# Turning the second pass's normed tiles through memory and VectorE, with both writes of a unit's attention weights issued before both reads

## Chip, cores, metric

The kernel runs on one core of one Trainium2 chip. The metric is device time in microseconds, the median of three runs of the kernel before.

## What is computed

Two layers run one after the other over 8 images of 32 x 32 positions and 512 channels, all in f32.

```python
# layer 0
x_norm = _group_norm(x, gn_scale, gn_bias).reshape(b, seq, c)
q, k, v = jnp.split(x_norm @ w_qkv + b_qkv, 3, axis=-1)      # 8 heads of 64
weight = softmax(einsum('bhld,bhsd->bhls', q * scale, k * scale))
x = x_flat + einsum('bhls,bhsd->bhld', weight, v) @ w_out + b_out
# layer 1, deformable attention; x_flat has rows of 512 positions of the turned image
q = layernorm(x, ln_g, ln_b).transpose(0, 3, 1, 2).reshape(b, h * w, c) @ wq + bq
offsets = pointwise(gelu(depthwise 7x7, stride 2, of q))     # 16 x 16 points an image
interp = grid_sample_bilinear(x, reference points + tanh(offsets))
k = v = interp.reshape(b, hg * wg, c) @ wv + bv
att = softmax((q @ mq) (k @ mk)^T) (v @ mv)                  # 8 heads, 256 keys
z = att @ mo_w + mo_b + x
out = gelu(layernorm(z, ln_g, ln_b) @ mlp_w + mlp_b) + z
```

## The kernel before, in words

The kernel has two passes. The first, up to about 2216 us of the span, is layer 0 and most of the depthwise convolution. The change is in the second pass, which is layer 1.

**Units.** The second pass has 64 units. Unit n is one pair of heads of one half image: 512 queries in four tiles of 128, against 256 keys. Four units make a half image, eight an image. `unit_steps` lists a unit's work:

- `scores`: the score matmuls (`sc<-keys,q`), the row maxima on VectorE (`nmax`), and eight exponentials on ScalarE (`e`);
- `moved`, for each of the two heads: VectorE turns the weights in 32 x 32 blocks (`sq<-e`). SP writes them to a buffer in memory (`sq_d<-sq`), and reads them back in the order in which they are the right operand (`et<-sq_d`). Before the change one head's write and read are issued together;
- `share` and `spread`: the reciprocals of the sums, sent through memory (`rs_d`, `inv`);
- `query_step`: the projection of the next unit's queries (`hat_h,wqq`) and its bias on ScalarE (`q`);
- `product`, about one unit later: the weighted values (`av<-et,vals`), and then `scale` on VectorE (`attH`).

**Back steps.** When a half image's four units are done, `back_steps` takes its four tiles through the output, one tile a unit. `fetch` and `add` bring the residual (`xr`). `joined` projects the attention (`mm<-wo,attH`), adds the residual on VectorE (`z`) and takes mean and variance (`stats`, `mv`). `norm` makes `zn`. `turned` transposes `zn` with four TensorE transposes into a PSUM tile, and ScalarE copies that to `zT` in two halves. `mlp` multiplies by `wm`, `biased` adds the bias on VectorE (`res`), `gelu` and `end` follow a unit or two later.

**Beside them.** The rest of the depthwise convolution lies in units 1 to 38: `fill` on TensorE (`mm<-wq_r,hat`), `pad` on VectorE, and taps in two lanes. Lane 0's taps (`chunk<-pad,dww`) run on VectorE, three or five to a unit; lane 1's on ScalarE and GpSimd. Once an image, `point_steps` works out the sampling corners (22 small VectorE operations, at the end of the units with n mod 8 = 3), gathers rows by GpSimd's indirect DMA, and mixes them on VectorE (`smp`, at the end of n mod 8 = 4 and 6). The keys and values of the next image follow on TensorE around n mod 8 = 7, 0 and 1.

**Order.** Every step is put down with `at(place, step)`, where a place is a unit's number and a fraction. `run_due` runs them by place, and `InOrder` keeps each engine's instructions in that order. So SP, too, issues in the order of the places, and waits at each DMA for what that DMA needs. A tile of a pool can only be written again when its last reader is done. `et` has two buffers, so a read of unit n waits for the product of unit n-1.

For a tile in the back steps the places before the change are: `joined` n+0.012, `norm` n+0.03, `turned` n+0.6, `mlp` n+1.03, `biased` n+1.0392. `moved` stands at n+0.02 and n+0.04, `share` at n+0.039, `spread` at n+0.041, `query_step` at n+0.042, `product` at n+1.1, `scale` at n+1.2. TensorE's order in a unit is therefore scores, `wo`, `wm` (of the tile before), queries, `av` (of the unit before), transposes of `zn`.

Of the kernel before, what the change touches and what calls it, by code (L numbers as in the profile page):

```python
# [9 lines left out]
F32 = mybir.dt.float32  # L10
# [7 lines left out]
P = 128  # L18
# [3 lines left out]
C = 512  # L22
NC = C // P
NT = S // P
QB = 512
NQB = S // QB
NQT = QB // P
NH = 8
HD = 64
NHP = NH // 2  # L30
GRP = 16
G = 16
NS = G * G
KS = 7
SQ = 32
NSQ = P // SQ
# [30 lines left out]
class Attention:  # L67
# [66 lines left out]
    def moved(self, u, h):  # L134

        nc, shape = self.nc, [P, NSQ, NS // P, NQT, SQ]
        sq = self.work.tile(shape, F32, tag="sq", name="sq", bufs=2)
        nc.vector.transpose(
            sq.rearrange("p s j i q -> p i (s j) q"),
            u["e"][h].rearrange("p (i b q) -> p i b q", i=NQT, q=SQ),  # L140
        )
        there = self.dram.tile([P, NSQ, NS // P * QB // NSQ], F32, tag="sq_d", name="sq_d", bufs=4)
        nc.sync.dma_start(there, sq.rearrange("p s j i q -> p s (j i q)"))
        u["et", h] = self.work.tile(shape, F32, tag="et", name="et", bufs=2)
        nc.sync.dma_start(
            u["et", h].rearrange("p r j i q -> p r (j i q)"),
            there.rearrange("(r k) s x -> (k s) r x", r=NSQ),
        )
# [93 lines left out]
def attention_then_deformable_attention(  # L242
# [30 lines left out]
    nc = tc.nc  # L273
# [4 lines left out]
    dram = ctx.enter_context(tc.tile_pool(name="dram", bufs=1, space=DRAM))  # L278
# [4 lines left out]
    ident = const.tile([P, P], F32, tag="ident", name="ident")  # L283
# [7 lines left out]
    def mm_tile():  # L291
        return ps_mm.tile([P, QB], F32, tag="mm", name="mm")
# [4 lines left out]
    def load_w(pool, w, name):  # L297
        t = pool.tile([P, NC, w.shape[1]], F32, tag=name, name=name)
        nc.sync.dma_start(t, by_chunk(w))
        return t  # L300
# [61 lines left out]
    def at(place, step):  # L362
        due.append((place, len(due), step))
# [37 lines left out]
    with ExitStack() as l0:  # L401
# [3 lines left out]
        nc = InOrder(tc)  # L405
# [46 lines left out]
        att = MovedAttention(nc, ident, ps_mm, ps_sc, ps_av, work, dram, 1)  # L452
# [336 lines left out]
        for b in range(B):  # L789
# [22 lines left out]
            for hp in range(NHP):  # L812
                for qt in range(NT):
                    n = first + hp * NT + qt
# [22 lines left out]
    with ExitStack() as l1:  # L837
        nc = tc.nc
# [22 lines left out]
        def load_small():  # L861
            with nc.allow_non_contiguous_dma(reason="small vectors onto partitions"):
                for t, v in (
                    (bvk, mk_b), (bv_c, bv), (bvv, mv_b), (bqq, mq_b), (bq_c, bq), (lng, ln_g),
                    (lnb, ln_b),
                ):
                    nc.sync.dma_start(t, v.rearrange("(c p) -> p c", p=P))

        def load_conv():
            with nc.allow_non_contiguous_dma(reason="small vectors onto partitions"):  # L870
# [222 lines left out]
        def query_step(hi, hp):  # L1093
            q = queries[hi, hp] = work.tile([P, QB], F32, tag="q", name="q")
            ps = project(lambda c: wqq[:, c, ts(hp, P)], lambda c: hat[hi][:, c, :])
            nc.scalar.activation(q, ps, AF.Identity, bias=bqq[:, hp : hp + 1])

        def tmp(name, bufs):
            return work.tile([P, C], F32, tag=name, name=name, bufs=bufs)

        def back_steps(hi, start, step, tail=False):

            b, half = divmod(hi, 2)
            xs = mid[b].rearrange("(t p e) c -> e t p c", e=2, p=P)[half]
            outs = out_tok[b].rearrange("(t p e) c -> e t p c", e=2, p=P)[half]
            xr, z, zn, zT, res = {}, {}, {}, {}, {}
            n_units = 2 * B * NHP

            def fetch(t):
                xr[t] = tmp("xr", 4)  # L1110
                nc.sync.dma_start(xr[t], xs[t])

            def add(t):
                nc.gpsimd.tensor_tensor(xr[t], xr[t], bo_row, ALU.add)

            def joined(t):
                ps = project(lambda c: attH[hi][:, c, ts(t, P)], lambda c: wo[:, c, :])
                z[t] = tmp("z", 4)
                nc.vector.tensor_tensor(z[t], ps, xr[t], ALU.add)
                stats = work.tile([P, 6], F32, tag="stats", name="stats")  # L1120
                mv = xr["mv", t] = work.tile([P, 3], F32, tag="mv", name="mv")
                nc.vector.bn_stats(stats, z[t])
                nc.vector.bn_aggr(mv[:, 0:2], stats)
                rstd(mv[:, 2:3], mv[:, 1:2], 1e-5)

            def norm(t):
                zn[t], mv = tmp("zn", 2), xr["mv", t]
                nc.vector.tensor_scalar(
                    zn[t], z[t], mv[:, 0:1], mv[:, 2:3], ALU.subtract, ALU.mult
                )  # L1130

            def turned(t):
                ps = mm_tile()
                for c in range(NC):
                    nc.tensor.transpose(ps[:, ts(c, P)], zn[t][:, ts(c, P)], ident)
                zT[t] = tmp("zT", 2)
                for half in range(2):
                    nc.scalar.copy(zT[t][:, ts(half, C // 2)], ps[:, ts(half, C // 2)])

            def mlp(t):  # L1140
                res["ps", t] = project(lambda c: zT[t][:, ts(c, P)], lambda c: wm[:, c, :])

            def biased(t):
                res[t] = tmp("res", 3)
                nc.vector.tensor_tensor(res[t], res["ps", t], bm_row, ALU.add)

            def gelu(t):
                nc.scalar.activation(res[t], res[t], AF.Gelu)

            def end(t):  # L1150
                (nc.vector if tail else nc.gpsimd).tensor_tensor(res[t], res[t], z[t], ALU.add)
                (nc.sync if tail else nc.gpsimd).dma_start(outs[t], res[t])

            for t in range(NC):
                over, eve = (start + step * t >= n_units - i and not tail for i in range(2))
                n, pair = start + step * t, start + step * (t - t % 2)

                ends = (n + 0.6, n + 1.03, n + 1.0392)
                if eve:
                    ends = (n + 0.61, n + 0.72, n + 0.73) if over else (n + 1.06, n + 1.62, n + 1.625)  # L1160
                places = (pair - 1.6, pair - 0.5), (n + 0.012, n + 0.03), ends
                if tail:
                    turn = n + 0.15 + 0.005 * (t > 0)
                    places = (n - 0.7, n - 0.6), (n, n + 0.01), (turn, n + 0.25, n + 0.26)
                steps = (fetch, add), (joined, norm), (turned, mlp, biased)
                for place, what in zip(sum(places, ()), sum(steps, ())):
                    at(place, lambda t=t, what=what: what(t))


                ends = [t - 1, t] if t % 2 and not tail else [t] if tail else []  # L1170

                for what, after in (
                    (gelu, 0.27 if tail else 0.735 if over else 1.72),
                    (end, 0.28 if tail else 0.74 if over else 2.24),
                ):
                    for i in ends:
                        at(n + after, lambda i=i, what=what: what(i))
# [4 lines left out]
        def unit_steps(n):  # L1182
            hi, hp = divmod(n, NHP)
            b = hi // 2
            u = dict(tiles=NQT, at=0, v=lambda j, h: vals[b][:, j, ds((2 * hp + h) * HD, HD)])

            def scores():
                u["q"], u["k"] = queries.pop((hi, hp)), keys[b][:, hp, :]
                u["e"] = att.scores(u)

            def scale():
                if hp == 0:
                    attH[hi] = work.tile([P, NHP, QB], F32, tag="attH", name="attH")
                att.scale(attH[hi][:, hp, :], u["inv"])

            at(n, scores)
            at(n + 0.02, lambda: att.moved(u, 0))
            at(n + 0.039, lambda: att.share(u["sums"]))
            at(n + 0.04, lambda: att.moved(u, 1))
            at(n + 0.041, lambda: u.update(inv=att.spread()))  # L1200
            last = n + 1 == 2 * B * NHP
            at(n + (1.3 if last else 1.1), lambda: att.product(u))
            at(n + (1.305 if last else 1.2), scale)
            if not last:
                at(n + 0.042, lambda: query_step(*divmod(n + 1, NHP)))

# [41 lines left out]
        def load_late():  # L1250
            nonlocal bq_row, wo, wm, bo_row, bm_row
            bq_row = load_row(wp, bq, "bq_row")
            wo = load_w(late2, mo_w, "wo")
            wm = load_w(late2, mlp_w, "wm")
            bo_row = load_row(late, mo_b, "bo_row")
            bm_row = load_row(late2, mlp_b, "bm_row")
            load_conv()
# [66 lines left out]
```

## Time and profile before

| | us |
|---|---|
| runs (median; lowest, highest) | 3404.53; 3399.92, 3406.07 |
| the profiled execution's own time | 3397.38 |
| its span, first to last instruction | 3395.7 |
| second pass, first scores to last instruction | 2216.1 to 3395.7 |
| TensorE busy / VectorE / ScalarE / GpSimd | 3298.7 / 2480.5 / 1811.4 / 1547.6 |
| granted TensorE clock, mean | 0.990 |

The profiled execution took 1.7 us more than its span, and lies 7.2 us under the median of the runs. A row of the profile's groups gives the line, engine, operation, output and inputs, the count, then busy time in us and mean ns of one, then the idle time before them and what ended it. Nearly every instruction stands under L54, the line of the recording helper, so that rows are told apart by the tiles. A matmul of 64 output rows runs beside its partner of the other 64, so the mean ns of one is more than the time until the next pair starts. That spacing is read from the timeline.

### The profile page before, as it was taken

The page shows a single profiled execution, that of the slowest core. Times are in us where ns is not written, and L with a number is a line of the kernel's source. Part 1 is how long each engine was busy: PE and PEld are TensorE (multiplying, and loading weights), DVE is VectorE, ACT ScalarE, POOL GpSimd, SP SyncE. Part 2 cuts the span into 40 slices and gives each one's busy share as a digit, 9 for nine tenths or more (in the row PEclk, how much of TensorE's full clock was granted, in tenths as well). Part 3 has the DMA queues.
Part 4 walks back from the last instruction along what each step waited for, and adds up shares of the span by engine and source line. Part 5 has one row for each costly group of instructions (what it writes and reads, how often), then busy time and mean ns, then how long its engine had stood idle before and what let it go on. Part 6 is the DMA issues. An engine that isn't in the chain of part 4 may idle for free. (4 is left out here: it accounts for less than half of the span.)

```text
span 3395.7 us, 59693 instructions
## 1 busy us (share of the span) xinstructions
PE 3298.7 (97%) x21736; PEld 1348.9 (40%) x21736; DVE 2480.5 (73%) x3373; ACT 1811.4 (53%) x3927; POOL 1547.6 (46%) x1903
## 2 busy tenths in 40 slices
PE   7999999999999999999999998889999999999998
PEld 3344444444344444344344343433333333333332
DVE  5776788888888888888898885157767586664654
ACT  3443365576576566566567561245565555554442
POOL 1002226656746746755755763215455354631322
PEclk9999999999999999999999999899999999999999
DMA  5666766766766766776767667446566565665653
GB/s 153 177 179 164 210 179 196 215 176 183 228 181 184 218 187 180 210 202 179 216 185 187 202 191 205 138 159 200 185 203 197 183 203 185 208 214 191 215 177 126
DMA packets 446645, 642.57 MB, mean 189 GB/s; under 512 B 77104, under 2 KB 240944, under 8 KB 444304
## 3 DMA queue, kind: packets, MB, share of 16 engines
q1 hardware_dynamic: 415712, 536.67, 54.5%
q0 software_dynamic: 29488, 100.00, 9.6%
q8 instruction: 172, 2.82, 0.3%
q10 hardware_dynamic: 1152, 2.10, 0.2%
q14 instruction: 121, 0.99, 0.1%
HBM read 246.38 MB, written 123.73 MB: 109 GB/s over the span
## 5 line engine op out<-in xcount | busy, mean ns | idle before, releaser
L54 ACT ACTIVATE e<-sc,nmax 128x1024 f32<-128x1024 f32 (+1 forms) x1024 | 803.4, 798 | 490.7 <-DVE nmax L54 487.9
L54 DVE TENSOR_REDUCE nmax<-sc 128x1 f32<-128x1024 f32 (+1 forms) x640 | 751.7, 1215 | 337.0 <-PE sc L54 333.0
L54 POOL TENSOR_TENSOR oa<-part_x,oa 128x256 f32<-128x256 f32 x852 | 640.7, 752 | 552.6 <-ACT part_x L54 506.3
L54 DVE STREAM_TRANSPOSE sq<-e 128x1024 f32<-128x1024 f32 x640 | 766.2, 1228 | 156.6 <-ACT e L54 125.1
L54 ACT ACTIVATE part_x<-pad_x,dww_x 128x256 f32<-128x256 f32 x852 | 442.3, 547 | 251.8 <-POOL oa L54 250.7
L54 PE MATMUL sc<-k,q 64*64 64x512 f32 x4096 | 516.6, 602 | 13.5 <-ACT e L54 10.3
L54 PE MATMUL av<-et,v 128*64 128x256 f32 x4096 | 502.5, 388 | 14.1 <-DMA et<-sq 12.5
L54 PE MATMUL mm<-xT,wqkv 128*64 128x512 f32 x2048 | 463.1, 594 | 3.2 <-issue 3.2
L54 PEld LDWEIGHTS av<-et,v 128*64 128x64 f32 x4096 | 275.4, 137 | 332.0 <-issue 170.3
L54 POOL TENSOR_TENSOR chunk<-parts,chunk 128x256 f32<-128x256 f32 x240 | 186.8, 778 | 277.3 <-ACT parts L54 263.4
L54 POOL TENSOR_TENSOR mv<-mv,minus_half 128x1 f32<-128x1 f32 x128 | 76.5, 598 | 510.3 <-DVE mv L54 509.8
L54 PEld LDWEIGHTS sc<-k,q 64*64 64x64 f32 x4096 | 139.2, 132 | 322.1 <-issue 204.0
L54 PEld LDWEIGHTS mm<-xT,wqkv 128*64 128x64 f32 x2048 | 148.3, 138 | 255.0 <-issue 239.6
L54 DVE SCALAR_TENSOR_TENSOR od<-pad_x,dww_x,od 128x256 f32<-128x256 f32 x276 | 232.2, 841 | 5.5
L54 PE MATMUL mm<-wo,attH 128*64 128x512 f32 x1024 | 234.8, 598 | 0.7 <-DVE attH L54 0.7
L54 PE MATMUL mm<-w,attT 128*64 128x512 f32 x1024 | 231.5, 596 | 2.0 <-DVE attT L54 2.0
L54 PE MATMUL mm<-wqkv,xT 128*64 128x256 f32 x2048 | 232.1, 379 | 0.0
L54 PE MATMUL mm<-wm,zT 128*64 128x512 f32 x1024 | 230.7, 592 | 1.0 <-ACT zT L54 1.0
L54 PE MATMUL mm<-hat_h,wqq 128*64 128x512 f32 x1024 | 230.8, 593 | 0.0
L54 ACT ACTIVATION_READ_ACCUMULATOR e<-sc,nmax 128x1 f32 x1024 | 209.3, 204 | 0.0
L54 ACT ACTIVATE parts<-pad,dww 128x256 f32<-128x256 f32 x240 | 126.4, 552 | 124.8 <-POOL chunk L54 124.4
L54 PEld LDWEIGHTS mm<-wqkv,xT 128*64 128x64 f32 x2048 | 148.1, 137 | 77.6 <-issue 6.4
(164 smaller groups left out, 3390.9 us busy)
## 6 DMA issues: line engine op xcount, KB each, us to landing
et<-sq SPq DMA_DIRECT2D x2048, 128.0 KB
sq_d<-sq SPq DMA_DIRECT2D x128, 512.0 KB
et<-sq_d SPq DMA_DIRECT2D x128, 512.0 KB
inv<-rs_d SPq DMA_DIRECT2D x256, 128.0 KB
hat_h<-hat_d SPq DMA_DIRECT2D x16, 1024.0 KB
xr<-mid SPq DMA_DIRECT2D x64, 256.0 KB
x<-in_x_dram POOLq DMA_DIRECT2D x60, 256.0 KB
out_dram<-res POOLq DMA_DIRECT2D x60, 256.0 KB
```

What stands on the lines that cost most here:

```text
L54: return self.tc.keep_in_program_order(op(*args, **kwargs))
```

## The change

The tiles of `zn` no longer go to TensorE, except in the last two tiles of the last-but-one half image and the last half image (`eve` or `tail`). `away` writes a tile to a buffer in memory in blocks of 128 channels, `back` reads it with four tokens of one block of channels to a partition, and `blocks` turns it on VectorE in 32 x 32 blocks, with steps of four elements in and out. A channel then lies at 4p+c and no longer at 128c+p, so `wm`, `lng` and `lnb` are loaded in that order, and the old `turned` takes its columns with a step of four. `moved` is split: the reads become `taken`, and both stand after both writes. `query_step` moves ahead of `mlp`.

```diff
@@ Attention.moved
-        there = self.dram.tile([P, NSQ, NS // P * QB // NSQ], F32, tag="sq_d", name="sq_d", bufs=4)
+        there = u["there", h] = self.dram.tile(
+            [P, NSQ, NS // P * QB // NSQ], F32, tag="sq_d", name="sq_d", bufs=4
+        )
         nc.sync.dma_start(there, sq.rearrange("p s j i q -> p s (j i q)"))
+
+    def taken(self, u, h):
+        there, shape = u["there", h], [P, NSQ, NS // P, NQT, SQ]
         u["et", h] = self.work.tile(shape, F32, tag="et", name="et", bufs=2)
-        nc.sync.dma_start(
+        self.nc.sync.dma_start(
@@ load_small
-                    (bvk, mk_b), (bv_c, bv), (bvv, mv_b), (bqq, mq_b), (bq_c, bq), (lng, ln_g),
-                    (lnb, ln_b),
+                    (bvk, mk_b), (bv_c, bv), (bvv, mv_b), (bqq, mq_b), (bq_c, bq),
                 ):
                     nc.sync.dma_start(t, v.rearrange("(c p) -> p c", p=P))
+                for t, v in ((lng, ln_g), (lnb, ln_b)):
+                    nc.sync.dma_start(t, v.rearrange("(p c) -> p c", p=P))
@@ back_steps
+            def away(t):
+                zn["d", t] = dram.tile([NSQ, P, P], F32, tag="zn_d", name="zn_d", bufs=3)
+                nc.sync.dma_start(
+                    zn["d", t].rearrange("r p x -> p r x"),
+                    zn[t].rearrange("p (r x) -> p r x", r=NSQ),
+                )
+
+            def back(t):
+                zn["l", t] = tmp("zn", 2)
+                nc.sync.dma_start(
+                    zn["l", t],
+                    zn["d", t].rearrange("r (q t) x -> (r q) (t x)", t=NSQ),
+                )
+
+            def blocks(t):
+                zT[t] = tmp("zT", 2)
+                nc.vector.transpose(
+                    zT[t].rearrange("p (c q t) -> p t c q", c=NC, q=SQ),
+                    zn["l", t].rearrange("p (t i c) -> p t c i", t=NSQ, i=SQ),
+                )
+
             def turned(t):
                 ps = mm_tile()
+                mixed = zn[t].rearrange("p (i c) -> p c i", c=NC)
                 for c in range(NC):
-                    nc.tensor.transpose(ps[:, ts(c, P)], zn[t][:, ts(c, P)], ident)
+                    nc.tensor.transpose(ps[:, ts(c, P)], mixed[:, c], ident)
...
-                ends = (n + 0.6, n + 1.03, n + 1.0392)
+                ends = (n + 0.0301, n + 0.0405, n + 1.013, n + 1.03, n + 1.0392)
...
-                steps = (fetch, add), (joined, norm), (turned, mlp, biased)
+                turns = (turned,) if eve or tail else (away, back, blocks)
+                steps = (fetch, add), (joined, norm), (*turns, mlp, biased)
@@ unit_steps
             at(n + 0.04, lambda: att.moved(u, 1))
-            at(n + 0.041, lambda: u.update(inv=att.spread()))
+            at(n + 0.0401, lambda: att.taken(u, 0))
+            at(n + 0.041, lambda: att.taken(u, 1))
+            at(n + 0.0411, lambda: u.update(inv=att.spread()))
...
-                at(n + 0.042, lambda: query_step(*divmod(n + 1, NHP)))
+                at(n + 0.014, lambda: query_step(*divmod(n + 1, NHP)))
@@ load_late
-            wm = load_w(late2, mlp_w, "wm")
+            wm = late2.tile([P, NC, C], F32, tag="wm", name="wm")
+            nc.sync.dma_start(wm, mlp_w.rearrange("(p c) o -> p c o", p=P))
```

The order of the built program has these new places. In a unit TensorE has scores, `wo`, queries, `wm`, `av`. VectorE has the block turn (`zT<-zn`) between `mv` and the first `sq`; `res` keeps its place between `rsT` and the second `sq`. SP has `sq_d`, `zn_d`, `rs_d`, `sq_d`, `et`, `zn`, `et`, `inv`, `inv`.

## Prediction

> **What bounds the kernel now.** I read the busy shares by stretch first, then one unit's timeline by engine, then the waits of the second pass, then its groups.
>
> ```profile
> core 0: us, PE busy (x) PEld busy (x) DVE busy (x) ACT busy (x) POOL busy (x), PEclk, DMA share, GB/s
> ...
> 2433.00:2615.00 182.00, 179.44 (x1098) 67.52 (x1099) 130.47 (x208) 104.40 (x285) 99.39 (x117) 1.00 0.62 197
> ...
> 3214.00:3324.00 110.00, 110.00 (x700) 42.03 (x699) 60.95 (x91) 52.59 (x153) 27.91 (x31) 1.00 0.58 190
> ```
>
> TensorE has hardly a gap at full clock; VectorE works 72% of a stretch with convolution taps and 55% of one without. The timelines of a unit without taps, TensorE first, then VectorE:
>
> ```profile
> 3294.69 1.96 PE L54 MATMUL sc<-keys,q 64*64 64x256 f32 x32
> 3296.57 3.65 PE L54 MATMUL mm<-wo,attH 128*64 128x512 f32 x16
> 3300.06 3.60 PE L54 MATMUL mm<-wm,zT 128*64 128x512 f32 x16
> 3303.49 3.60 PE L54 MATMUL mm<-hat_h,wqq 128*64 128x512 f32 x16
> 3306.93 1.89 PE L54 MATMUL av<-et,vals 128*64 128x512 f32 x8
> 3308.74 0.66 PE L54 MATMUL mm<-ident,zn 128*128 128x128 f32 x4
> ```
>
> ```profile
> 3300.35 0.69 DVE L54 TENSOR_TENSOR z<-mm,xr 128x512 f32<-128x512 f32 x1 [1.29 <-PE mm L54]
> ...
> 3302.10 1.25 DVE L54 STREAM_TRANSPOSE sq<-e 128x1024 f32<-128x1024 f32 x1
> ...
> 3304.06 0.65 DVE L54 TENSOR_TENSOR res<-mm,bm_row 128x512 f32<-128x512 f32 x1
> 3304.62 1.24 DVE L54 STREAM_TRANSPOSE sq<-e 128x1024 f32<-128x1024 f32 x1
> 3308.89 0.69 DVE L54 TENSOR_TENSOR attH<-av,inv 128x512 f32<-128x512 f32 x1 [3.03 <-PE av L54]
> ```
>
> A unit lasts 14.64 us (3294.69 to 3309.33), all of it TensorE. `wm` starts 5.4 us after the scores and waits for nothing that VectorE does in this unit. The waits from 2280 to 3350 us, TensorE's and SP's:
>
> ```profile
> SPq L54 <- DMA sq_d<-sq: 532.0, 121, 9.8
> ...
> PEld av L54 <- DMA et<-sq_d: 40.1, 18, 7.2
> ```
>
> SP stands half of the time before a read whose write has not landed, and only then issues the second head's write. In 18 places this reaches TensorE, at the product: 40.1 us.
>
> **The part taken away.** With transposes, the next scores start 2.40 us after `av` (3306.93 to 3309.33). Where a projection follows, `av` holds the array 1.72 us (key, value and convolution units show it). So four transposes cost between 0.59 us (3308.74 to 3309.33, should scores pay the same change of tiles) and 0.68. I take 0.64: 58 tiles x 0.64 = -37 us. The 116 ScalarE copies (0.37 us each) go too, 43 us, off the path: ScalarE is half idle. Each of the 58 units is then 14.0 us long if nothing is late.
>
> **The writes ahead of the reads.** The second read now follows the first by 0.8 us of issue (the `zn` read between them), where today it follows a write's landing, 4.5 us. The first read moves behind `rs_d` and the second write, but in quiet units it can't go sooner anyway: its buffer comes free when `av` ends, at the unit's end. Some 36 of the 40.1 us should go; about 4 stay in the first units (around 2280 to 2304), where the first head's read is itself late. This holds only if the second `sq` isn't made late, which comes next.
>
> **What takes its place.** `wm` now stands after the queries, 8.8 us after the scores, and needs the block turn of the same unit. That stands on VectorE behind `nmax`, `z` and the statistics. `res` has kept its place ahead of the second `sq` but must wait for a `wm` that ends 12.4 us after the scores, not 8.9. So the second `sq` (and its write, both reads and `inv` on SP), `attH`, the taps and the next `nmax` queue behind TensorE, and TensorE's next `wm` behind them. That is a closed loop, worked out from the spacings of the timeline's rows: `wm` to `res` 3.65, `res` 0.57, `sq` 1.16, `attH` 0.60, two `nmax` 2.27, `z` to statistics 1.74 (3300.35 to 3302.10), block turn 0.71, hand-over 0.1 = 10.8 us. TensorE's own round is 14.0. In a quiet unit 3.2 us are spare; in another, taps, corners and samples lie in the loop.
>
> The block turn itself (128x512) has no row. The nearest:
>
> ```profile
> L54 DVE STREAM_TRANSPOSE sq<-e 128x1024 f32<-128x1024 f32 x120 | 148.8, 1240 | 47.2 <-ACT e L54 35.7 <-issue 6.8 <-DMA xr<-mid 3.6
> ...
> L54 DVE SCALAR_TENSOR_TENSOR chunk<-pad,dww,chunk 128x256 f32<-128x256 f32 x140 | 108.9, 778 | 3.8
> ...
> L54 DVE STREAM_TRANSPOSE rsT<-rs 128x32 f32<-128x32 f32 x60 | 12.7, 212 | 2.1
> ```
>
> A line through 1024 elements at 1.24 and 32 at 0.21 gives 0.71 at 512. But it steps by four f32, in and out. Here the Trainium skill ("SBUF — State Buffer", section on the port map) speaks against the change: memory lines are 16 bytes, and every access that crosses to a new line pays; this one crosses at each element. No VectorE row here steps so far in SBUF. On ScalarE, `k` (step of four, from PSUM) takes 684 ns and `q` (step of one) 683. I take 0.71, the nearest row, and keep 1.25, half the rate, as the other end (rival 2 has the sum); a gain is excluded, since nothing stood there before.
>
> TensorE's wait per unit, loop minus 14.0, with the extra VectorE work read from its timeline between the second `sq` and the next `nmax`:
> - n mod 8 = 4: corners 3.6 us and three taps 2.25 make 16.65, so 2.6; units 12, 20, 28, 36: 10.6. Without taps (44, 52) 0.4 each: 0.8.
> - n mod 8 = 5: samples and three taps. Unit 21: 3.4 + 3.1, so 3.3; 29: 3.1; 37: 3.7; 13: the rows land late (last at 2436.5), 5.2. Sum 15.3.
> - n mod 8 = 6, five taps 3.9: 0.6 and 0.7 (22, 30): 1.3.
> - n mod 8 = 7: samples and three taps, stretched beside GpSimd's work. Unit 23: 5.1 + 5.5, so 7.4; 31: 6.2 + 5.0, so 8.0; 15: 4.5 + 2.0, so 3.3; 39: 6.2 and no taps, 3.0; 7, where rows land late, 4.3. Sum 26.
> - n mod 8 = 0 to 3: nothing; keys, values or fills lengthen TensorE's round by 2 to 9 us, or only three taps lie in it.
>
> **The DMAs.** A tile adds a write and a read of 256 KB: 30 MB, and two issues of some 0.4 us on SP, which waits anyway. The read stands behind the second `sq_d` write and the first `et` read, and must have landed 8.1 us after the next scores. SP's timeline shows write and read of a quiet unit, then of a crowded one (`xr` ahead, `out_dram` beside it):
>
> ```profile
> 3303.37 0.33 SPq L54 DMA_DIRECT2D sq_d<-sq  x1
> 3308.84 0.38 SPq L54 DMA_DIRECT2D et<-sq_d  x1
> ...
> 3184.84 0.36 SPq L54 DMA_DIRECT2D sq_d<-sq  x1
> 3194.93 0.37 SPq L54 DMA_DIRECT2D et<-sq_d  x1
> ```
>
> Quiet: `sq` ends 0.2 us into the next unit, the `zn` read is issued at 1.4. In the chain of waits an `et` read takes 4.1 to 4.6 us, of which 512 KB at the 367 GB/s of the busiest slice (DMA view, 3214 to 3324) are 1.4. The queue drains two and a half such from 2 us on, with 1 us to land: about 6.5 us into the unit, an estimate. In time by 1.6. Crowded: the first write lands 10 us after issue, the read is issued near 6.2 and lands past 11. Going by today's landing times, units 45, 46, 47, 53 and 55 pay 1.8 + 2.1 + 1.4 + 0.9 + 4.0 = 10.2 (elsewhere VectorE is later still). The Trainium skill ("DMA: Bandwidth & Descriptors", "Anatomy of one DMA") gives 2.0 us plus bytes at 436 GB/s, its fit for GpSimd's path: 2.6 us for 256 KB, an estimate from it, and then nothing lands late and the sum is 10.2 lower. The rows (4.1 to 4.6, and up to 10) decide.
>
> `query_step` ahead of `mlp`: `q` is ready 3.4 us sooner, covered either way. GpSimd's queue keeps its order. `wm`, `lng` and `lnb` in a new order: loaded once behind the weight products, zero; six tiles still transpose on TensorE with a step of four: 24 instructions, four tiles in the tail, 0 to +2 us.
>
> **Sum.** -37 - 36 + (10.6 + 0.8 + 15.3 + 1.3 + 26 + 10.2 = 64) = -9 us against the profiled execution's own 3397.4: 3388.4. That execution lies 7.2 us under the median, so 3395.5; I say 3395.
>
> **The rivals.**
> 1. *The read of `zn` becomes the bound: slower.* If it lands later than 8.1 us after the scores in quiet units, `wm` starts late by the excess in each of some 37 units not already late. It decides from 1.6 us beyond my 6.5; at 2.6 beyond, +37: -9 + 37 = +28, 3432. For: it is last of 1.3 MB in one burst, and crowded landings take 10 us. Against: DMA is busy only 58 to 62%.
> 2. *The block turn runs at half rate.* +0.54 in each of the 21 or so waiting units, +12: +3, 3407, no change. In quiet units it ends at 8.65, still in time.
> 3. *The closed loop costs half.* If samples find their rows landed, and GpSimd's turns don't stretch the taps (5.5 us for three in unit 13, 2.2 in 19), 32 of the 64 go: -41, 3363.
> 4. *The second half of the title does nothing*: the second `sq` ends three microseconds later in quiet units, so the second read gains little there. The product's waits lie in the other units, so this alone takes back at most 20: +11, 3415.
>
> **How the numbers follow.** The sum (own range 3380 to 3412) has 0.43; rival 1 0.18, rival 2 0.15, rival 3 0.17, rival 4 0.07. About 0.2% (7 us) is what a measurement of this kernel tells from no change. Faster: 0.43 x 0.55 + 0.17 + a little of rival 2 = 0.42. Same: 0.43 x 0.3 + half of rival 2 = 0.20. Slower: the rest, 0.38. The range, 3363 to 3432, runs from rival 3 to rival 1.
>
> **What would show it.** Right: quiet units of 14.0 us; `av` waits for `et` nearly gone; a new wait of TensorE for `zT` of about 60 us, in n mod 8 = 4, 5 and 7; `res` waiting on TensorE some 2 us in most units; block turn near 0.7 us. Wrong: a block turn of 1.2 us (rival 2); VectorE waiting for the `zn` read in units 57 to 61 (rival 1); `zT` waits under 35 us (rival 3); 20 us or more left at `av` (rival 4).

## Result and the profile after

| | before | after |
|---|---|---|
| runs: median (lowest, highest), us | 3404.57 (3395.51, 3408.95) | 3414.62 (3409.56, 3426.21) |
| ratio, 95% interval | | 1.0039 (1.0026, 1.0051) |
| the profiled execution's own time; its span | 3397.38; 3395.7 | 3417.55; 3415.8 |
| second pass in the profiled execution | 1179.6 | 1193.0 |
| TensorE busy; VectorE busy | 3298.7; 2480.5 | 3271.9; 2556.7 |
| granted clock, mean | 0.990 | 0.984 |

The changed kernel is 0.39% slower, 13 us by the ratio (the medians are 10 us apart), where 9 us less was forecast. The profiled executions differ by 20.1 us, but 6.7 of these are there before the second pass begins, in a first pass that is the same program but for the order of three loads; over all the executions profiled here the first pass ends anywhere from 2212.6 to 2225.2 us. The second pass is 13.4 us longer, and that is what has to be explained.

Busy time by stretch, the same two stretches as before. The columns are TensorE, its weight loads, VectorE, ScalarE, GpSimd, then the granted clock and the DMA share:

```profile
core 0: us, PE busy (x) PEld busy (x) DVE busy (x) ACT busy (x) POOL busy (x), PEclk, DMA share, GB/s
2433.00:2615.00 182.00, 164.25 (x962) 60.84 (x964) 136.47 (x205) 88.93 (x244) 88.22 (x105) 0.95 0.66 211
3214.00:3324.00 110.00, 108.72 (x695) 42.05 (x693) 66.90 (x98) 44.21 (x135) 25.19 (x28) 1.00 0.71 229
```

The stretch without taps is still all TensorE. In the stretch with taps TensorE now stands 18 us out of 182, and its granted clock there fell from 1.00 to 0.95. That second number was in no part of the prediction.

A quiet unit after, TensorE's timeline:

```profile
3331.40 1.96 PE L54 MATMUL sc<-keys,q 64*64 64x256 f32 x32
3333.29 3.65 PE L54 MATMUL mm<-wo,attH 128*64 128x512 f32 x16
3336.78 3.60 PE L54 MATMUL mm<-hat_h,wqq 128*64 128x512 f32 x16
3340.21 3.60 PE L54 MATMUL mm<-wm,zT 128*64 128x512 f32 x16
3343.64 1.89 PE L54 MATMUL av<-et,vals 128*64 128x512 f32 x8
3345.46 1.74 PE L54 MATMUL sc<-keys,q 64*64 64x256 f32 x28
```

and VectorE's, around it:

```profile
3329.81 0.69 DVE L54 TENSOR_TENSOR res<-mm,bm_row 128x512 f32<-128x512 f32 x1 [2.04 <-PE mm L54]
3330.41 1.24 DVE L54 STREAM_TRANSPOSE sq<-e 128x1024 f32<-128x1024 f32 x1
3331.57 0.67 DVE L54 TENSOR_TENSOR attH<-av,inv 128x512 f32<-128x512 f32 x1
3333.41 2.36 DVE L54 TENSOR_REDUCE nmax<-sc 128x4 f32<-128x1024 f32 x2 [1.17 <-PE sc L54]
3336.99 0.69 DVE L54 TENSOR_TENSOR z<-mm,xr 128x512 f32<-128x512 f32 x1 [1.22 <-PE mm L54]
...
3338.74 1.16 DVE L54 STREAM_TRANSPOSE zT<-zn 128x512 f32<-128x512 f32 x1
```

From scores to scores it is 14.06 us (3331.40 to 3345.46), where it was 14.64. The block turn ends at 3339.90, and `wm` starts at 3340.21: 0.3 us are left. The second `sq` now starts behind `res`, and `res` behind `wm`.

The waits of the second pass from 2280 to 3350 us, first SP's, then those of the engines:

```profile
SPq L54 <- DVE sq L54: 574.2, 112, 12.9
SPq L54 <- DMA sq_d<-sq: 97.5, 72, 3.9
```

```profile
DVE res L54 <- PE mm L54: 104.8, 55, 3.9
...
PE mm L54 <- DVE zT L54: 44.0, 20, 6.0
...
PEld mm L54 <- DVE attH L54: 18.9, 7, 5.0
...
PE mm L54 <- DVE attH L54: 13.2, 4, 4.1
...
PEld av L54 <- DMA et<-sq_d: 0.8, 1, 0.8
```

The 40.1 us of `av` for `et` are gone, as meant. In their place TensorE waits for VectorE's `zT` and `attH`. VectorE in turn waits 104.8 us for `wm` before `res`. The two engines wait for each other.

The block turn's group shows the duration that the prediction had to bound:

```profile
L54 DVE STREAM_TRANSPOSE zT<-zn 128x512 f32<-128x512 f32 x58 | 66.3, 1143 | 1.4 <-DMA zn<-zn_d 1.4
```

1143 ns, not 710. The read of `zn` is late twice in 58, by 1.4 us in all.

A second thing on VectorE got longer. Three of the four instructions that mix the samples, in unit 21 and then in unit 45:

```profile
2600.10 7.43 DVE L54 SCALAR_TENSOR_TENSOR smp<-row,wt,smp 128x512 f32<-128x512 f32 x3
...
3056.98 2.33 DVE L54 SCALAR_TENSOR_TENSOR smp<-row,wt,smp 128x512 f32<-128x512 f32 x3
```

In unit 21 GpSimd's own additions lie beside 6 us of them, in unit 45 beside none. From 2280 us to 3350 these instructions are busy for 66.0 us after the change and 42.4 before it (53.3 with the writes' order alone), while their waits for rows that have not landed fell from 12.8 us to nothing. The change sets the samples behind `res` and so to another time, beside GpSimd's work in units 21, 29 and 37 (7.4 us each). That GpSimd is what stretches them is read from the overlap and was not tried.

### The profile page after: what moved, and what is told of

It is laid out like the page before. It is cut to its first block, busy times and chain, and to the rows that moved or that the text cites. A ratio compares the mean times of both kernels' runs of the same rounds, so it can differ in the third digit from the quotient of the medians.

```text
span 3415.8 us, 59420 instructions
## 1 busy us (share of the span) xinstructions
PE 3271.9 (96%) x21504; PEld 1330.3 (39%) x21504; DVE 2556.7 (75%) x3431; ACT 1776.7 (52%) x3811; POOL 1543.0 (45%) x1903
## 5 line engine op out<-in xcount | busy, mean ns | idle before, releaser
L54 PE MATMUL sc<-k,q 64*64 64x512 f32 x4096 | 515.8, 602 | 13.4 <-ACT e L54 10.3
L54 PE MATMUL mm<-wm,zT 128*64 128x512 f32 x1024 | 244.0, 620 | 48.1 <-DVE zT L54 47.1
L54 PE MATMUL mm<-wo,attH 128*64 128x512 f32 x1024 | 236.8, 602 | 13.3 <-DVE attH L54 13.2
```

The costliest lines, as they stand in the source:

```text
L54: return self.tc.keep_in_program_order(op(*args, **kwargs))
```

## Experiments

Ratios are to the kernel before, run on the same chip, with 95% intervals; 0.001 is 3.4 us. Each kernel differs from the changed one, or from the one before, by the few lines shown.

### The two halves apart

`writes_only` is the kernel before, with the reads taken out of `moved`:

```diff
+            at(n + 0.0401, lambda: att.taken(u, 0))
+            at(n + 0.041, lambda: att.taken(u, 1))
-            at(n + 0.041, lambda: u.update(inv=att.spread()))
+            at(n + 0.0411, lambda: u.update(inv=att.spread()))
```

> The kernel before, with the second half of the change alone: both writes of a unit's weights are issued ahead of both reads, TensorE still turns the normed tiles. Theory A (each half is worth what it takes away: the reads no longer stand before the second write, 36 of the 40.1 us that the product waits for et go; of these the pair of PE and its loads waits together, so 25 to 36 us of time): 3404.6 - 30 = about 3375, waits of the product for et under 8 us. Theory B (the writes' order gives nothing, because the product's waits have another cause, such as DMA landing times): 3404.6 within 7 us, waits for et still near 30 us. If B holds, the whole of the loss after the change is the turn's.

Measured: 0.9946 (0.9928, 0.9964), 18 us faster (12 to 25). Its waits:

```profile
PE mm L54 <- DVE zn L54: 5.2, 5, 1.3
PE mm L54 <- DVE res L54: 5.0, 4, 1.6
...
PEld av L54 <- DMA et<-sq_d: 3.1, 2, 2.2
...
PE av L54 <- DMA et<-sq_d: 2.9, 2, 1.5
```

Theory A for the waits: those for `et` fall from 40.1 to 3.1 us, so all that was named goes. The time does not follow in full; 25 to 36 us had been expected. In the units with samples TensorE now waits 10 us for `zn` and `res` (1.8 before), where the waits for `et` had stood before. The lengths of the units in the two profiled executions agree: units 45, 46, 47 and 55 lost 6.8 us of waits and are 7.5 us shorter, units 21, 29, 31, 37 and 39 lost 7.2 us and are 0.6 us shorter. That the one covered the other is read from the places of the units, not tried.

`turn_only` is the changed kernel with each read next to its own write:

```diff
-            at(n + 0.0401, lambda: att.taken(u, 0))
+            at(n + 0.0302, lambda: att.taken(u, 0))
-                ends = (n + 0.0301, n + 0.0405, n + 1.013, n + 1.03, n + 1.0392)
+                ends = (n + 0.0301, n + 0.0403, n + 1.013, n + 1.03, n + 1.0392)
```

> The changed kernel with the second half undone: each head's read stands right behind its own write again (the zn write and the zn read are ahead of the read that would hold them up). Theory A (the halves add up; the turn frees 34 us of TensorE but ties wm to VectorE of the same unit, about 69 us of waits and some 10 to 15 us of half clock behind them): 3414.6 + 30 = about 3445, with waits of TensorE for zT of 45 us or more and waits of the product for et of 25 us or more. Theory B (the turn itself is near neutral and the loss comes from the crowded SP queue): 3405 to 3415. Theory C (the waits for zT swallow those for et, since wm is late in the same units): 3420 to 3430.

Measured: 1.0108 (1.0089, 1.0127), 37 us slower. That is A's time within its interval, with waits of 48.6 us for `zT`, but 10.6 us (and 13.0 of the loads) for `et`, less than A said: some of C. The halves nearly add up: -18 + 37 = +19 against 13 measured. The loss is the turn's, and it hides a gain. The new place of `query_step` goes with the turn here; `turn_some_dense2` below shows that it costs nothing by itself (a quiet unit with the queries ahead and TensorE's transposes lasts 14.64 us there, as before the change).

### The block turn's step

`turn_dense` lays `zn_d` by token group, so that both sides of the block turn step by one element (the write of `zn` becomes four DMAs of 32 partitions, and `wm`, `lng` and `lnb` are loaded to match; not shown):

```diff
-                    zT[t].rearrange("p (c q t) -> p t c q", c=NC, q=SQ),
-                    zn["l", t].rearrange("p (t i c) -> p t c i", t=NSQ, i=SQ),
+                    zT[t].rearrange("p (c t q) -> p t c q", c=NC, q=SQ),
+                    zn["l", t].rearrange("p (t c i) -> p t c i", t=NSQ, i=SQ),
```

> The changed kernel, with a block turn that steps by one element in and out: memory holds the tile so that the read is plain, wm and the two LayerNorm vectors are loaded in the order that this gives, and the write of zn is four DMAs of 32 partitions. Theory A (the step of four f32 costs): the block turn takes 0.7 us in place of 1.14; in some 21 units where TensorE waits for zT it ends 0.43 sooner, about -9 us: 3405. Theory B (the size decides, not the step, the line through the shapes of one step being wrong): the turn stays near 1.1 us and the time at 3414.6. Theory C (the step costs, but the end of the wait is set by the read of zn or by SP's queue, with three more issues on it): 0.7 us a turn and a time within 3 us of 3414.6 or above it.

Measured: 1.0016 (1.0006, 1.0026), 8 us better than the changed kernel. The row:

```profile
L54 DVE STREAM_TRANSPOSE zT<-zn 128x512 f32<-128x512 f32 x58 | 40.7, 702 | 2.3 <-DMA zn<-zn_d 2.3
```

Theory A, in both numbers: 702 ns, and 9 us forecast. The step of four f32 costs 0.44 us a turn, 1.63 times as long for the same elements. It is about a quarter of the turn's loss (8 of 32 to 37 us) and not its main cause.

### What ties TensorE to VectorE

`res_later` moves the bias add behind the second `sq` and the samples; `mlp_last` moves `wm` behind the product as well, and the bias add behind attH and lane 0's taps:

```diff
-                ends = (n + 0.0301, n + 0.0405, n + 1.013, n + 1.03, n + 1.0392)
+                ends = (n + 0.0301, n + 0.0405, n + 1.013, n + 1.03, n + 1.0416)   # res_later
+                ends = (n + 0.0301, n + 0.0405, n + 1.013, n + 1.15, n + 1.4)      # mlp_last
```

> The changed kernel with the bias add of wm (res) behind the second sq and the samples on VectorE, wm where it was. Theory A (the loop wm, res, second sq, attH is the cost, as the prediction's sum of 10.8 us has it): VectorE does the second sq (1.2) and the samples (5 to 6) beside wm (3.65) in place of after it, 2 to 4 us in each of some 18 late units: 3414.6 - 45 = about 3370, ratio 0.991. Theory B (attH, which needs av behind wm on TensorE, closes the loop just as well; only samples gain, in 12 units): about -15, ratio 1.000. Theory C (the place of res is of no weight): 1.004.

> The changed kernel with wm moved behind the product on TensorE (order: scores, wo, queries, av, wm) and its bias add on VectorE moved behind the second sq, attH and the taps of lane 0. So the second sq, the samples and attH no longer stand behind wm, and wm may start 1.9 us later without a wait. Theory A (the loop wm, res, second sq, attH, nmax, z, block turn makes the loss): the lateness of wm, 69 us summed over the units, and most of the half-clock stretches (54.6 us in the second pass after, 20.5 before) go; 3414.6 - 70 - 10 = about 3335, and quiet units stay at 14.06. Theory B (contention: VectorE's samples at 1.57 us in place of 1.01 and the DMA's 30 MB more make the loss): waits move to another place, 3405 to 3415. Theory C (half of it): 3375.

Measured: `res_later` 0.9994 (0.9982, 1.0006), `mlp_last` 0.9966 (0.9954, 0.9979). The first is theory B: 15 us, not 45; `attH` needs `av`, and `av` stands behind `wm`, so the loop closes without `res`. The second gains 25 us, a third of what A expected and less than C's 40. Theory A was too high in both, and the next pair shows what is left when `wm` no longer waits.

`mlp_next` gives TensorE the block turn of the unit before:

```diff
+                far = 1 if not tail and n < n_units - 3 else 0
+                if far:
+                    ends = (*ends[:3], n + 2.0125, n + 2.0392)
-                xr[t] = tmp("xr", 4)
+                xr[t] = tmp("xr", 8)
-                z[t] = tmp("z", 4)
+                z[t] = xr[t]
```

> The changed kernel with wm and its bias add moved one unit on (order on TensorE: scores, wo, wm of the tile whose block turn ended in the unit before, queries, av), gelu and the last add one unit on as well; z takes the place of xr in one ring of eight buffers. The block turn may then come 10.9 us later than in a quiet unit before TensorE waits, and VectorE still turns all 58 tiles. Theory A (it is the demand within the same unit that costs, not the turn's work on VectorE): the waits for zT go and 58 x 0.585 = 34 us of TensorE stay saved beside the writes' order, so 0.9946 of before less 34 us: about 3344 where before is 3398, or 0.984. Theory B (VectorE has too much work in the units with samples and corners, so the waits move to the scores, to attH or to av): near the order of writes alone, 0.993 to 0.998. Theory C (contention with 30 MB more on the DMA queues): product's waits for et come back, over 15 us.

Measured: 0.9945 (0.9926, 0.9965): theory B. The waits for `zT` fell to 3.1 us and nothing was won beyond the writes' order. TensorE's own waits:

```profile
PE mm L54 <- DVE attH L54: 18.2, 4, 4.5
PE av L54 <- DMA et<-sq_d: 8.0, 6, 1.9
PE mm L54 <- DVE res L54: 7.4, 3, 2.6
```

Now `wo` waits for `attH`, 4.5 us at a time, in units 13, 21, 29 and 37. There `attH` stands on VectorE behind the samples, and VectorE has 1.15 us of block turn more in every unit than it had.

`mlp_next_dense` takes the narrow step besides.

> The same, with the block turn that steps by one element (0.70 us in place of 1.14). Theory A (with wm one unit on the turn is hidden): the same as with the wide step within 4 us, about 0.984 of before. Theory B (VectorE is still the bound in the crowded units): 58 x 0.44 = 26 us less of VectorE's work brings another 8 us, as it did with wm in the same unit.

Measured: 0.9936 (0.9916, 0.9956), not to be told from `mlp_next`. Theory A's 0.984 is not reached, and whether the turn's length is hidden with `wm` a unit later stays open, as the 8 us of theory B lie within the intervals.

`mlp_next_smp` moves the first half's samples behind `attH`:

```diff
-            for h, (p0, p1) in enumerate(((-0.28, 0.0415), (1.72, 2.0415))):
+            for h, (p0, p1) in enumerate(((-0.28, 1.205), (1.72, 2.0415))):
```

> wm one unit on, as before it, and the samples of the first half of the points behind attH on VectorE. Theory A (with wm a unit on, what is left in units n mod 8 = 5 is wo waiting for attH, which stands behind 5 to 6 us of samples: 18 us of waits with 4 of them over 4 us, and the half clock after each): those waits fall below 5 us, 4 to 7 units gain 4.5 us each, 25 us: 0.9945 - 0.007 = 0.987 of before. Theory B (VectorE is simply full there, the lateness moves to nmax, q or the next wm): 0.993 to 0.995.

Measured: 0.9894 (0.9868, 0.9920), 17 us better than `mlp_next` and nearer to A's 0.987 than to B. The four waits for `attH` are gone and units 13, 21, 29 and 37 are 4.2 to 5.7 us shorter. Part comes back elsewhere, as B has it, in units 22, 30 and 38 (2.5 to 3.4 us longer):

```profile
PE sc L54 <- ACT q L54: 19.3, 8, 4.2
PE mm L54 <- DVE res L54: 7.8, 4, 2.8
```

### The turn where VectorE has room

`turn_some` takes the turn through memory for the 32 tiles whose block turn falls in a unit without samples, corners or many taps; TensorE turns the rest:

```diff
+                free = not tail and ((n + 1) % 8 < 4 or n > 54)
+                if not free:
+                    ends = (n + 0.6, n + 1.03, n + 1.0392)
-                turns = (turned,) if eve or tail else (away, back, blocks)
+                turns = (turned,) if eve or tail or not free else (away, back, blocks)
```

> The changed kernel, where the turn through memory is taken only by the 32 tiles whose block turn falls in units without corners, samples or five taps ahead of it (n mod 8 = 0 to 3, and all from unit 56 on); TensorE turns the others as before the change. Theory A (the loss sits in the units where VectorE has more work, n mod 8 = 4, 5, 7, and elsewhere a tile saves 0.585 us): the writes' order alone less 32 x 0.585 = 19 us: 0.9946 - 0.0055 = 0.989 of before, waits for zT under 6 us. Theory B (the turn costs in every unit through the queues and the clock): no better than the writes' order alone, 0.9946 or above.

Measured: 0.9884 (0.9862, 0.9907), where A said 0.989; TensorE waits 3.1 us for `zT`. Length of a unit against `writes_only`, mean over units 8 to 39, from the starts of the scores in the profiled executions, us:

| n mod 8 | 0 to 3 | 4 | 5 | 6 | 7 |
|---|---|---|---|---|---|
| the changed kernel | -0.6 | +2.5 | +4.5 | -0.8 | +5.2 |
| `mlp_next` | -0.6 | -0.6 | +4.8 | -0.9 | +1.3 |
| `mlp_next_smp` | -0.6 | -0.6 | +0.1 | +1.5 | +0.3 |
| `turn_some` | -0.4 | +0.1 | +1.3 | -0.2 | -1.8 |

The first row is the answer to where the gain went. In the quiet units the turn pays what it frees, and three kinds of unit in eight take back more.

`turn_some_dense` and `turn_some_dense2` add the narrow step. In the former the tiles that TensorE turns bring their channels in another order than `wm` has its rows, so it is read for its time alone; in the latter VectorE's `zn` lays them right.

> The turn through memory for the 32 tiles of quiet units alone, with the block turn of step one (0.70 us). Theory A (in quiet units the block turn ends in time either way): the same as with the wide step, 0.988 within 0.001. Theory B (lateness builds up over quiet units as well, or VectorE's time counts in the units behind): 32 x 0.44 = 14 us of VectorE's work bring 4 us or more, 0.987 or below.

> turn_some_dense with the channels of the tiles that TensorE turns laid in the order of wm's rows (in turn_some_dense these 20 or so tiles met the rows in another order, a difference of values, not of work; here VectorE's norm writes them in 32-channel pieces). Theory A: 0.986 to 0.988 of before, about 3357. Theory B (the norm in pieces is slow, on the path of TensorE's transposes): above 0.990.

Measured: 0.9856 (0.9827, 0.9884) and 0.9890 (0.9875, 0.9905). The first would be theory B, the second is the same as the wide step and lies between its own two theories. The second passes of the two profiled executions are equally long (1138.2 us), so what sets the two ratios apart is not shown to be in the second pass, and a gain from the narrow step is not shown. `turn_some_dense2`, at a median of 3358.68 where the kernel before has 3397.02, and `turn_some` beat the kernel before by about 1.1% and the changed kernel by 1.5%. TensorE's waits in the former:

```profile
PE mm L54 <- DVE attH L54: 5.3, 4, 1.4
PE sc L54 <- ACT q L54: 3.8, 1, 3.8
PE mm L54 <- DVE rs L54: 2.9, 3, 1.0
PE mm L54 <- DVE zT L54: 2.7, 1, 2.7
```

### The clock behind a wait

Unit 15 of the changed kernel, VectorE's timeline and then TensorE's:

```profile
2481.78 6.56 DVE L54 SCALAR_TENSOR_TENSOR smp<-row,wt,smp 128x512 f32<-128x512 f32 x3
2488.27 0.68 DVE L54 TENSOR_TENSOR attH<-av,inv 128x512 f32<-128x512 f32 x1
...
2490.51 2.35 DVE L54 TENSOR_REDUCE nmax<-sc 128x4 f32<-128x1024 f32 x2
...
2494.51 1.13 DVE L54 STREAM_TRANSPOSE zT<-zn 128x512 f32<-128x512 f32 x1
```

```profile
2486.19 3.60 PE L54 MATMUL mm<-hat_h,wqq 128*64 128x512 f32 x16
2495.78 6.06 PE L54 MATMUL mm<-wm,zT 128*64 128x512 f32 x16 [5.99 <-DVE zT L54]
2501.66 1.90 PE L54 MATMUL av<-et,vals 128*64 128x512 f32 x8
```

The samples hold up `attH`, two taps and the maxima behind it, then the block turn; `wm` starts 6.0 us late. It then takes 6.06 us for what took 3.60 in the quiet unit. The granted clock (1.00 is full speed), last but two in these rows, over the wait and over `wm`:

```profile
2486.20:2495.80 9.60, 3.61 (x20) 1.04 (x16) 9.43 (x13) 4.58 (x18) 4.00 (x5) 0.90 0.81 255
2495.80:2501.70 5.90, 5.90 (x18) 1.94 (x20) 2.19 (x4) 2.23 (x5) 2.97 (x4) 0.59 0.39 136
```

The clock does not fall after every wait. `wm` of units 12 and 20 waited equally long:

```profile
2434.65 5.35 PE L54 MATMUL mm<-wm,zT 128*64 128x512 f32 x16 [2.31 <-DVE zT L54]
...
2594.17 3.65 PE L54 MATMUL mm<-wm,zT 128*64 128x512 f32 x16 [2.31 <-DVE zT L54]
```

What decides can be read from the traces. In each of the 15 traces kept the second pass's half-clock stretches start on a grid with a step of 3.413 us: their starts lie whole steps apart, to within 0.01 us. The steps of this grid around the two waits (the first number after the length is TensorE's busy time):

```profile
2432.40:2435.82 3.42, 1.17 (x6) 0.57 (x8) 3.35 (x6) 3.42 (x13) 0.91 (x3) 1.00 0.99 343
2435.82:2439.23 3.41, 3.41 (x10) 1.20 (x8) 1.08 (x3) 2.10 (x5) 3.18 (x5) 0.50 1.08 352
...
2589.42:2592.83 3.41, 2.43 (x12) 0.57 (x8) 3.31 (x6) 2.68 (x12) 1.97 (x3) 1.00 0.88 249
2592.83:2596.24 3.41, 2.07 (x10) 0.92 (x12) 3.38 (x6) 2.95 (x10) 1.65 (x3) 1.00 0.91 335
```

Unit 12's wait lies inside one step, which is busy to 0.34, and the next step runs at 0.50. Unit 20's wait lies across two, busy to 0.71 and 0.61, and the clock stays full. Over the 15 traces, from the second pass's first half-clock step to 3350 us, a full-clock step that was less than 0.40 busy was followed by half clock 78 times in 78, and one that was more than 0.46 busy never (4640 steps). After a half-clock step that was more than 0.8 busy the clock was full again 88 times in 88. So, as an estimate from these figures, one wait in full work that is longer than 4.1 us (twice 0.6 of a step) always costs half clock, one shorter than 1.8 us (0.54 of a step) never does, and between them it depends on where the wait falls.

From 2280 us to 3350 the trace has the clock at 0.5 for 51 us after the change and for 19 before it. TensorE was busy in 41.4 and 10.5 of these, so some 15 us more were lost (half the difference), an estimate. To see whether it is real time, TensorE's idle time was filled with matmuls of no use:

```diff
+                for i in range({12: 5, 13: 6, 15: 12, ...}.get(start + step * t + 1, 0)):
+                    for half in (ds(0, HD), ds(HD, HD)):
+                        nc.tensor.matmul(ps[half], lhsT=wm[:, i % NC, half], rhs=wm[:, i % NC], start=True, stop=True)
```

> The changed kernel with idle time of TensorE filled: in nine units whose wm waits for zT (12, 13, 15, 20, 23, 28, 31, 36, 39) 5 to 12 pairs of matmuls on wm alone, of 0.43 us a pair and so a little shorter than the wait read from the trace of after (2.3 to 6.0 us), go into the same PSUM tile ahead of the true ones, which then start it anew. They do no useful work. Theory A (the wait also lowers the granted clock, and the matmuls after it run at half of it): wm takes 3.65 us in units 12, 15, 23, 31 and 39 in place of 5.35 to 6.06, half-clock stretches fall from 54.6 us to near 25, and the time falls by some 10 us: 3404, ratio 1.001. Theory B (the slow matmuls have another cause, such as reads of zT or contention on memory, or their time is given back later): wm stays at 5.4 to 6 us there, time at 3414 or above it by what the filler costs where it is too long.

Measured: 1.0052 (1.0036, 1.0067). `wm` is back at 3.60 us in all nine units, as theory A has it, but the fillers were twice as long as meant and held `wm` up, so the time does not decide between them; `after_filled_half` has them half as long.

> The changed kernel with TensorE's idle time filled, as in after_filled, with half as many matmuls: there a pair took 0.86 us and not 0.43, so wm began 1.8 to 4.1 us later than zT allowed in the nine units (24 us in sum), and yet the second pass grew by 7.8 us only. Now 2, 3 or 6 pairs, 1.7, 2.6 and 5.2 us against waits of 2.3, 2.7 to 3.4, and 6.0. They do no useful work. Theory A (half clock after the wait costs time of its own): the time falls under that of after by the longer matmuls, some 10 to 15 us, 1.000 +- 0.001 of before; units 15, 23 and 31 end 2.4 us sooner each. Theory B (the slow matmuls are made up for later, since the next wait ends when VectorE is ready): wm back at 3.65 us, and the time at 1.004 all the same.

Measured: 1.0031 (1.0020, 1.0042). The interval takes in the changed kernel's 1.0039 and theory B's 1.004, and leaves out theory A's 1.000 +- 0.001: the whole does not show a gain. Unit 15 does:

```profile
2487.72 5.32 PE L54 MATMUL mm<-wm 128*64 128x512 f32 x24
2493.62 3.65 PE L54 MATMUL mm<-wm,zT 128*64 128x512 f32 x16 [0.58 <-DVE zT L54]
2497.11 1.89 PE L54 MATMUL av<-et,vals 128*64 128x512 f32 x8
```

`wm` starts 14.7 us after the scores (15.0 in the changed kernel) and takes 3.65 us, not 6.06. Unit 15 ends 2.7 us sooner, 23 and 31 by 2.4 and 2.3, 39 by 1.8, 12 by 1.8. Unit 13 is 5.6 us longer in this execution: its samples take 7.5 us in place of 4.1, and `wo` waits 4.1 us for `attH` behind them. So the half clock is shown to cost about 2 us in each of five units, 11 in all, in one execution against one (units 12 and 39, with waits of 2.3 and 3.4 us, could have escaped it by their place on the grid; 15, 23 and 31 could not). That its sum reaches the median is not shown.

## Why the prediction was wrong, point by point

**TensorE's share.** 0.64 us a tile was forecast, 0.585 came (14.64 to 14.06), the lower of the two ends that the prediction had: 34 us, not 37.

**The writes ahead: the step most off.** "Some 36 of the 40.1 us should go" is right of the waits (3.1 us are left) and wrong of the time: `writes_only` gained 18 us. Part of these waits stood over other lateness, VectorE's in the units with samples, which showed as soon as they were gone (0.6 us gained for 7.2 us of waits in five such units). The prediction credited each wait at its full length and asked what is late next only for the first units.

**The closed loop.** Right in mechanism and place, and its sum came close in part by luck. `wm`'s lateness beyond 8.8 us after the scores, summed over the units, is 69 us, where 64 was forecast. By kind: n mod 8 = 4, 11.1 for 11.4; 7, 25.5 for 26; 6, 0.2 for 1.3; 5, 24 for 15.3; units 45, 46, 47 and 53 to 55, 5.8 for 10.2; unit 6, 2.4, which was not in the sum. But only 44.0 us of it are TensorE's waits for `zT`, where about 60 was named as the sign. Another 13.2 are waits of `wo` for `attH`, which the sum didn't have (4.0 to 4.1 us in units 21, 29 and 37, 1.0 in 13), and some 8 are matmuls at half the clock behind them. In those three units the samples were priced at about 3.4 us and took 7.9. `res` in the loop was only half right: `res_later` shows that `attH`, behind `av`, ties it as well. And some lateness was there with the writes' order alone, so that it can't all be laid on the turn.

**Late reads of `zn`, 10.2 us.** Wrong, and with them rival 1: VectorE waits 1.4 us for that read in the whole pass; it lands 5.0 us after its issue (median). The units named do pay 5 us, through VectorE. The size of the landings was taken from crowded units, and it did not hold for this read.

**The block turn.** The nearest row gave 0.71, true of the step of one (0.702). The step of four takes 1.143, so rival 2 was nearly right. The rule of the Trainium skill ("SBUF — State Buffer", section on the port map), that an access pays when it crosses to a new line of 16 bytes, pointed the right way against the row. The ScalarE rows that spoke against it, `k` and `q`, read from PSUM, and said nothing of SBUF. The half rate was priced at +12, and going back to the narrow step brought 8.

**The clock.** Not in the sum at all: about 11 us by the units, 15 by the estimate, though no run shows the whole becoming faster without it. The Trainium skill has the rule ("TensorE: Matmul & The Clock Gate", "What's actually happening"): half clock after an idle window of about 3.4 us. The 6.0 us waits agree; unit 12's wait of 2.3 us fills no such window and by the rule alone would cost nothing, but `wm` took 5.35 us behind it: a step of the grid that is busy to 0.34 is enough, and the measurement decides. The prediction, which had waits of up to 8 us in its own list, had no term for what follows them.

**Sum.** Half by half: -9 was -36 (writes) and +27 (turn). Measured: -18 and +32, the latter from 1.0039/0.9946. So 18 of some 22 us lie in the writes, and 5 in the turn: there 3 us less saved, 5 us more of lateness and the unpriced clock stand against the lateness that the writes' order has without any turn. How much each of these is worth was not measured apart. The split also depends on the order: with the turn first (+37, `turn_only`) the writes then bring 24 us, and the misses are 12 in the writes and 10 in the turn. The writes' gain is the larger miss either way, and at half its size it was enough to turn the sign: with 36 there and 32 for the turn, the sum would have been -4.

**The rivals.** 3 (half the loop) is false by the 69 us, and by the 44.0 us of waits for `zT`, where its sign was under 35. 4 (the writes do nothing) is false by `writes_only` and by the 3.1 us left at `av`, though half of the gain did stay away.

## What to carry to other kernels

In this kernel, work that left the bound engine paid only where the engine that took it had slack between the last input and the first reader; ask that of each kind of unit, not of the mean busy share (VectorE 72% here, and full where the samples lie). Taking the new path in the quiet units alone gained 39 us (18 of them by the order of the writes), where taking it everywhere lost 13. And when a wait is taken away, credit its time only after looking at which other engine is late in the same unit.

## What the runs showed of the hardware

- VectorE's 32x32 block transpose of 128x512 f32 takes 702 ns with a step of one element in and out, and 1143 ns with a step of four (16 bytes) on both sides.
- TensorE's granted clock fell to half on a grid of 3.413 us: after each of the 78 full-clock steps that were less than 0.40 busy, after none of the 4640 that were more than 0.46 busy (15 traces, second pass). The same wait of 2.31 us was followed by half clock in unit 12 (0.34 busy in its step) and by full clock in unit 20 (0.71 and 0.61).
- Three VectorE instructions that mix samples (128x512 f32) took 2.3 us in unit 45, with GpSimd idle beside them, and 7.4 us in unit 21, with GpSimd at work beside 6 us of them.
- One matmul call of 64 output rows shows as two matmul records (12 calls, 24 records), so that a pair of calls holds TensorE for 0.86 us (5.2 us for six pairs), not 0.43.
